# GAT's first edges by fp32 one-hots made from a broadcast of places, in blocks of 125 nodes and a written order

## The chip, the cores and the metric

The kernel runs on one core of one Trainium2 chip. The metric is the device time of one execution in microseconds (us), lower is better; where several runs are given, their median. The core has engines that run beside each other, each through its own queue in order: PE (matmuls, with its weight loads shown apart as PEld), DVE (elementwise and reductions), ACT (elementwise, with functions), POOL (here: indirect DMAs, that is gathers and scatters by a list of rows) and SP (here: only DMA issues). DMA queues of SP, ACT and POOL share 16 DMA engines. SBUF is the memory on the chip, PSUM the one that PE writes to.

## The reference

There are 3125 nodes with 64 features and 103125 edges (50000 random pairs in both directions and a loop for each node), sorted by destination. Two residual blocks follow one another, each on relu(layernorm(x)):

```python
def gin_layer(x, src, dst, ew, w1, b1, w2, b2):
    msg = x[src] * ew[:, None]
    agg = segment_sum(msg, dst)
    h = relu((agg + x) @ w1 + b1)
    return h @ w2 + b2            # three of these, relu between them

def gat(x, src, dst, W, a_src, a_dst, bias):
    xw = (x @ W).reshape(n, H, C)                 # H = 8 heads
    logits = leaky_relu(al_s[src] + al_d[dst], 0.2)   # al: xw times a_src or a_dst
    e = exp(logits - segment_max(logits, dst)[dst])
    alpha = e / segment_sum(e, dst)[dst]
    return segment_sum(alpha * xw[src], dst) + bias
```

In the second block x is embedded to 128 features (with a time embedding of node_vec), and three GAT layers follow (128 to 256, 256 to 256, 256 to 128), each with a dense residual, a batch norm over the nodes and a silu; a last matmul goes back to 64. Everything is fp32.

## The kernel before, in words

Nodes stand in NT = 25 blocks of P = 128 (3200 places for 3125 nodes). The program runs these stages one after another.

**search** and **slots** (L623, L749) sort the edges into slots: a row of slots for each destination. `weigh(t)` (L817) finds, for a block of destinations, which slots name the same source, adds up their weights and gives the first of them a cell in a dense adjacency of 3200 x 3200 fp32 in DRAM; `put(t)` (L836) has POOL scatter these values one column of 128 cells at a time (`scatter`, L941; 857 DMAs in the profile). Then, for each destination and each block of sources, the first edge is taken out (`tops`, L860 to L870) and its place within the block kept in `lane`; what is left of the edges goes into lists (`rank`, L711; the destinations in an order of falling list length, in `perm`, and the sources in `idx`). The lists' lengths per block are fixed: MORE = (44, 24, 22, 21, 20, 19, 18, 17, 17, 16, 16, 15, 15, 14, 14, 13, 13, 13, 12, 11, 11, 10, 10, 8, 7), 400 in all. A flag then selects `fast` (L1290).

**hots** (L923) makes the one-hots of the first edges: for each destination block t, DVE compares `lane` with a row of numbers (L929, bf16, 128 x 3200), PE transposes the 25 squares, ACT copies them from PSUM and SP writes 0.8 MB to `hot[t]` in DRAM. It stands before GIN in the text, but nothing keeps the scheduler from running it beside GIN.

**gin** (L954), three times: the adjacency (41 MB) is loaded in 75 pieces by SP (225 in all) and multiplied by the node features on PE (L977).

**gat** (L991), three times, with D = 256, 256 and 128. A preparation computes xw with the logits' source parts beside it (W = D + 8 columns), writes it to DRAM as `tab`, splits it into three bf16 terms that add up to the fp32 value (`split`: ACT one copy, DVE three operations per five blocks), and computes the dense residual into DRAM. `add_edges` (L1058) does the edges, in a loop over the destination blocks t:

- `gather(t, s0, n, rows)` (L1071): for each source block s, three bf16 matmuls with the one-hot as the stationary operand give in PSUM the row of xw that each destination's first edge names (L1078); ACT copies two of them at a time to SBUF (L1079). A 26th "source block" is an identity, for the node itself. The 26 are done as 12, 12 and 2, in three large tiles that rotate.
- `weigh(t)` (L1085) adds the logits, and `exps` (L1176) takes maximum, exponential (ACT, L1182) and sum. `add_part` (L1102) multiplies the rows by the exponentials (`times`, L1100), folds the 12 into 6 (L1105) and adds these up in PSUM with an identity matmul (L1107).
- `others(t)` (L1111) has POOL fetch the rows of the list, one indirect DMA of 128 rows for each list place (L950), into tiles of SG = 8 places, six of them in rotation. `add_others` (L1125) computes their logits (L1128), exponentials and products (L1100), sums all places in PSUM (L1139), and a scatter by POOL brings the sum to `more`, in the nodes' own order.

The lists are worked off in step with the blocks (`due`, a share of the list work by each t). The tile framework's scheduler decides the order on each engine. It places semaphores by the tiles' dependences, and a tile of a rotation can be written again when its last reader is done. `close_rows` (L1185) joins `res` and `more` by their maxima and sums, adds the dense part and applies batch norm and silu.

Of the kernel before, what the change touches and what calls it, by code (L numbers as in the profile page):

```python
# [22 lines left out]
NT = 25  # L23
NP = NT * P
# [573 lines left out]
class Fast(Base):  # L598
# [8 lines left out]
    def __init__(self, base, ctx):  # L607
        self.__dict__.update(base.__dict__)
        self.keep = ctx.enter_context(self.tc.tile_pool(name="keep", bufs=1))

        self.node = self.keep.tile([P, NT, 4], I32, name="node")
        self.place = self.keep.tile([P, NT], I32, name="place")
        self.flag = self.keep.tile([1, 1], I32, name="flag")

        self.bad = self.keep.tile([P, 8], F32, name="bad")
        self.edges = self.tc.dram_tile([P * J + P, 2], F32, name="edges")

        self.adj = self.tc.dram_tile([NP * NP + NC * P, 1], F32, name="adj")

        self.hot = self.tc.dram_tile([NT, P, NP], BF16, name="hot")  # L620
        self.adj_rows = self.adj[: NP * NP].rearrange("(s d) f -> s (d f)", d=NP)
# [89 lines left out]
    def rank(self, sp, ps, count, caps, bad):  # L711
# [12 lines left out]
        for c0 in range(0, BINS * NT, BLK):  # L724
            w = min(BLK, BINS * NT - c0)
            for lhs, o in ((self.after, ahead), (self.ones, tot)):
                pp = ps.tile([P, BLK], F32, name="pp", bufs=4)
# [21 lines left out]
    def slots(self):  # L749
# [11 lines left out]
        self.identb = keep.tile([P, P], BF16, name="identb")  # L761
        nc.vector.tensor_copy(self.identb, self.ident)
# [5 lines left out]
        with tc.tile_pool(name="slots", bufs=1) as sp, tc.tile_pool(name="slots_ps", bufs=1, space=PSUM) as ps:  # L768
# [35 lines left out]
            for t, c in enumerate(spans):  # L804
# [5 lines left out]
            earlier = sp.tile([P, CMAX, CMAX], F32, name="earlier")  # L810
            wide = [P, CMAX, CMAX]
            nc.vector.tensor_tensor(
                earlier, k[:, :, None].to_broadcast(wide), k[:, None, :].to_broadcast(wide), op=ALU.is_gt
            )
            celli, val = self.celli, self.val

            def weigh(t):  # L817
# [7 lines left out]
                    same, src[:, c, None].to_broadcast(wide), src[:, None, c].to_broadcast(wide), op=ALU.is_equal  # L825
                )
                nc.vector.tensor_tensor(part, same, earlier[:, :n, :n], op=ALU.mult)
                again = sp.tile([P, CMAX], F32, name="again", bufs=2)[:, :n]
                nc.vector.reduce_sum(again, part, axis=AX.X)
                nc.vector.scalar_tensor_tensor(again, again, 0.0, taken[:, c], op0=ALU.is_equal, op1=ALU.mult)  # L830
                nc.vector.tensor_tensor(again, again, cell[:, c], op=ALU.mult)
                nc.vector.tensor_tensor(celli[:, c], again, spare[:, c], op=ALU.add)
                nc.vector.tensor_tensor(same, same, wgt[:, None, c].to_broadcast(wide), op=ALU.mult)
# [16 lines left out]
            nc.gpsimd.iota(ends, pattern=[[P, NT]], base=P + 1, channel_multiplier=0, allow_small_or_imprecise_dtypes=True)  # L850
# [3 lines left out]
            nc.vector.tensor_mul(key, key, taken)  # L854
            NF = (NT + 7) // 8 * 8
# [6 lines left out]
            for t, c in enumerate(spans):  # L862
# [4 lines left out]
                    u, key[:, None, c].to_broadcast(wide), ends[:, :, None].to_broadcast(wide), op=ALU.is_lt  # L867
                )
                nc.vector.tensor_tensor(u, u, key[:, None, c].to_broadcast(wide), op=ALU.mult)
# [15 lines left out]
            pt = ps.tile([1, P], F32, name="pt1")  # L885
# [14 lines left out]
            lanes = sp.tile([P, NT, NF], F32, name="lanes")  # L900
            nc.sync.dma_start(lanes, tops_d.rearrange("(t p) f -> p t f", p=P))
# [4 lines left out]
            nc.gpsimd.iota(block, pattern=[[P, NT]], base=1, channel_multiplier=0, allow_small_or_imprecise_dtypes=True)  # L906
            nc.vector.tensor_copy(int_[:, :, :NT], lanes[:, :, :NT])
            nc.vector.tensor_scalar(int_[:, :, :NT], int_[:, :, :NT], SHIFT, None, op0=ALU.arith_shift_right)
            nc.vector.tensor_copy(self.lane, int_[:, :, :NT])
            nc.vector.tensor_sub(self.lane, self.lane, block[:, None, :].to_broadcast([P, NT, NT]))  # L910
            nc.vector.memset(self.void, 0.0)
            nc.vector.tensor_scalar(self.void[:, :, :NT], self.lane, 0.0, NEG, op0=ALU.is_lt, op1=ALU.mult)
# [7 lines left out]
            nc.vector.tensor_scalar(off, src, 0.0, float(NP + 1), op0=ALU.is_equal, op1=ALU.mult)  # L920
            nc.vector.scalar_tensor_tensor(self.idx, src, -1.0, off, op0=ALU.add, op1=ALU.add)

    def hots(self, pool, ps):  # L923

        nc = self.nc
        for t in range(NT):
            oh = pool.tile([P, NT, P], BF16, name="oh", bufs=2)
            wide = [P, NT, P]
            nc.vector.tensor_tensor(  # L929
                oh, self.lane[:, t, :, None].to_broadcast(wide), self.iota[:, None, :].to_broadcast(wide), op=ALU.is_equal  # L930
            )
            by_src = pool.tile([P, NP], BF16, name="by_src", bufs=2)
            for s0 in range(0, NT, 8):
                n = min(8, NT - s0)
                pt = ps.tile([P, 8, P], BF16, name="pt", tag="mm")
                for i in range(n):
                    nc.tensor.transpose(pt[:, i], oh[:, s0 + i], self.identb)
                nc.scalar.copy(by_src[:, s0 * P : (s0 + n) * P], pt[:, :n].rearrange("p s d -> p (s d)"))
            nc.sync.dma_start(self.hot[t], by_src)

    def scatter(self, table, rows, group="place"):  # L941
        for row, idx in rows:
# [3 lines left out]
            self.tc.declare_no_dep(st.ins, group=group, reason="each has a row of its own")  # L946
            self.tc.add_to_no_dep_group(group, st.ins)
# [43 lines left out]
    def gat(self, layer, K, D, xt, yt):  # L991
# [4 lines left out]
        tab = tc.dram_tile([NP + 1, W], F32, name=f"tab{layer}")  # L996
# [4 lines left out]
        with ExitStack() as ctx:  # L1001
            pool = ctx.enter_context(tc.tile_pool(name=f"gat{layer}", bufs=1))
            ps = ctx.enter_context(tc.tile_pool(name=f"gat_ps{layer}", bufs=2, space=PSUM))

            split = [pool.tile([P, NT, W], BF16, name=f"split{i}") for i in range(3)]
            ald = pool.tile([P, NT, H], F32, name="ald")
            stat = pool.tile([P, NT, 2 * H], F32, name="stat")
            back = pool.tile([P, NT, 2 * H], F32, name="back")
            gb, ab, bg, bb = (self.column(pool, name(n), KO) for n in ("gat_b", "adj_b", "bn_g", "bn_b"))
            bias = pool.tile([P, KO], F32, name="bias")  # L1010
            nc.scalar.dma_start(tab[NP:], self.none[:, 256 - D :])
            with tc.tile_pool(name=f"gat_a{layer}", bufs=2) as ap:
# [13 lines left out]
                for t0 in range(0, NT, S):  # L1026
                    row = ap.tile([P, S, W], F32, name="row")
                    for t in range(t0, t0 + S):
                        p = ps.tile([P, BLK], F32, name="pw", tag="mm")[:, : W + H]
                        for k in range(K):  # L1030
                            nc.tensor.matmul(p, xt[k][:, t * P : (t + 1) * P], gw[:, k], start=k == 0, stop=k == K - 1)
                        nc.scalar.copy(row[:, t - t0], p[:, :W])
                        nc.scalar.copy(split[0][:, t], p[:, :W])
                        nc.vector.tensor_copy(ald[:, t], p[:, W:])
                    nc.sync.dma_start(tab[t0 * P : (t0 + S) * P].rearrange("(t p) d -> p t d", p=P), row)
                    self.store_rows(ald_d, ald, t0, t0 + S)
                    left = ap.tile([P, S, W], F32, name="left", bufs=1)
                    part = [a[:, t0 : t0 + S] for a in split]
                    nc.vector.tensor_sub(left, row, part[0])
                    nc.vector.tensor_copy(part[1], left)  # L1040
                    nc.vector.tensor_sub(part[2], left, part[1])
# [11 lines left out]
            with tc.tile_pool(name=f"gat_sum{layer}", bufs=2) as io:  # L1053
                self.add_edges(io, ps, layer, D, xt, yt, split, ald, stat, tab, ald_d, res, more)
            with tc.tile_pool(name=f"gat_io{layer}", bufs=2) as io:
                self.close_rows(pool, io, ps, D, yt, stat, back, dense, res, more, bg, bb, xt[0])

    def add_edges(self, io, ps, layer, D, xt, yt, split, ald, stat, tab, ald_d, res, more):  # L1058
# [5 lines left out]
        two = xt[0].bitcast(BF16)  # L1064
        hot = [two[:, :NP], two[:, NP:], io.tile([P, NP], BF16, name="hot", bufs=1)]
        tiles = [a[:, : HALF * W].rearrange("p (s w) -> p s w", w=W) for a in (xt[1], yt[0], yt[1])]

        def load(t):
            nc.sync.dma_start(hot[t % 3], self.hot[t])

        def gather(t, s0, n, rows):  # L1071
            for i in range(0, n, 2):
                g = ps.tile([P, 2, BLK], F32, name="g", tag="g")
                for j in range(2):
                    s = s0 + i + j
                    one = hot[t % 3][:, s * P : (s + 1) * P] if s < NT else self.identb
                    for k, a in enumerate(split):
                        nc.tensor.matmul(g[:, j, :W], one, a[:, min(s, t) if s == NT else s], start=k == 0, stop=k == 2)  # L1078
                nc.scalar.copy(rows[:, i : i + 2], g[:, :, :W])  # L1079

        def parts(t):
            last = io.tile([P, 2, W], F32, name="last")
            return [(0, HALF, tiles[2 * t % 3]), (HALF, HALF, tiles[(2 * t + 1) % 3]), (2 * HALF, 2, last)]

        def weigh(t, now):  # L1085
            l = io.tile([P, NS, H], F32, name="l1")
            wide = [P, NS, H]
            nc.vector.tensor_tensor(
                l, self.void[:, t, :, None].to_broadcast(wide), ald[:, t, None, :].to_broadcast(wide), op=ALU.add
            )  # L1090
            for s0, n, rows in now:
                nc.vector.tensor_tensor(l[:, s0 : s0 + n], l[:, s0 : s0 + n], rows[:, :, D:], op=ALU.add)  # L1092
            self.lrelu(l, l)
# [260 lines left out]
```

## Time and profile before

| | us |
|---|---|
| median of 5 runs | 5112.81 (5109.6 to 5129.89) |
| the profiled execution, its own time | 5133.85 |
| its span in the profile | 5132.0 |
| POOL busy | 2686.1 (52%) |
| PE busy | 2240.1 (44%) |
| DVE busy | 2030.3 (40%) |
| ACT busy | 866.8 (17%) |
| moved by DMA | 465.63 MB, mean 91 GB/s |

The stages, from the start of the span: search and slots to about 894 (POOL's scatters go on to 1550), GIN from 1557 to 1979, GAT layers from about 2016 (edges 2064 to 3072, 3204 to 4200 and 4330 to 5075), the end at 5132.

How to read the profile: a row of groups gives line, engine, operation, output and inputs, their shapes and the count, then the busy time in us and the mean of one in ns, then the engine's idle time just before such operations and what ended most of it ("<-PE pa L1139": an operation of PE on tile `pa` at line 1139). A row of the stages gives the window, its length, and for each engine the busy time with the number of records, then the mean clock granted to PE as a share of the full one, the busy share of the DMA engines and the rate. A row of the timeline gives start, length, engine, line and operation, and in brackets the idle time before it. PE's records overlap each other, so that the mean duration of one is longer than the distance between two.

### The profile page before, as it was taken

What the parts mean: (1) busy time and instruction counts of PE and PEld (TensorE: products, weight loads), DVE (VectorE), ACT (ScalarE), POOL (GpSimd) and SP (SyncE); (2) the same over time, 40 slices, a digit from 0 to 9 for tenths busy, and PEclk for the clock granted to TensorE, in tenths of its full rate; (3) what the DMA queues carried; (4) which work ended last, traced back from release to release, by engine and by line L of the source; (5) the groups of instructions that cost most, each with busy time, mean ns of one, the idle gap of its engine ahead of it and who ended that gap; (6) DMA issues with size and microseconds to landing.
All of it is one profiled execution on the core that took longest, in us unless ns stands there. A gap on an engine that the chain in (4) does not pass through costs nothing. (4 is left out here: it accounts for less than half of the span.)

```text
span 5132.0 us, 36988 instructions
## 1 busy us (share of the span) xinstructions
PE 2240.1 (44%) x13235; PEld 1663.6 (32%) x13235; DVE 2030.3 (40%) x3336; ACT 866.8 (17%) x1812; POOL 2686.1 (52%) x2350
## 2 busy tenths in 40 slices
PE   0000000000007897466755566466665655364464
PEld 0000000000003433345544444345544544254454
DVE  3571930100005203345554445355554544243345
ACT  0000000000005302212212214122221214121122
POOL 2486687777770000565575440655565431666663
PEclk9555555555558997778877878778877877677787
DMA  9100000000007994432232223422322224322222
GB/s 382 51 1 7 1 0 14 2 1 1 1 0 264 363 377 160 113 86 86 84 94 77 74 62 128 100 81 85 89 86 83 64 73 127 52 76 70 69 75 70
DMA packets 235781, 465.63 MB, mean 91 GB/s; under 512 B 102719, under 2 KB 145858, under 8 KB 232386
## 3 DMA queue, kind: packets, MB, share of 16 engines
q1 hardware_dynamic: 113606, 252.99, 14.0%
q0 software_dynamic: 89424, 157.97, 12.5%
q10 hardware_dynamic: 32556, 52.20, 2.8%
q8 instruction: 106, 1.74, 0.1%
q14 instruction: 89, 0.73, 0.0%
HBM read 363.97 MB, written 99.01 MB: 90 GB/s over the span
## 5 line engine op out<-in xcount | busy, mean ns | idle before, releaser
L950 POOL DMA_INDIRECT rows<-tab,idx x1200 | 1467.4, 1223 | 867.0 <-PE pa L1139 510.4
L943 POOL DMA_INDIRECT adj<-val,celli x857 | 924.9, 1079 | 347.0 <-issue 259.9
L1078 PE MATMUL g<-split,xt 128*128 128x264 bf16 (+1 forms) x3825 | 506.8, 288 | 651.5 <-ACT xt L1079 399.3
L1078 PEld LDWEIGHTS <-xt 128*128 128x128 bf16 x3825 | 380.9, 109 | 769.3 <-issue 689.2
L1079 ACT COPY xt<-g 128x528 f32<-128x528 f32 (+1 forms) x900 | 465.4, 527 | 734.1 <-PE g L1078 288.6
L977 PE MATMUL pa<-adj_t,h 128*64 128x512 f32 (+1 forms) x1050 | 274.6, 560 | 667.0 <-DMA adj_t<-adj 666.6
L950 POOL DMA_INDIRECT at<-ald,perm x75 | 73.8, 984 | 924.7 <-DVE l L1092 532.5
L1139 PE MATMUL pa<-rows,ident 128*128 128x256 f32 (+1 forms) x2400 | 503.3, 365 | 42.3 <-ACT o L1140 25.1
L1128 DVE TENSOR_TENSOR l<-rows,at 128x64 f32<-128x64 f32 (+4 forms) x180 | 38.8, 216 | 1065.0 <-DMA rows<-tab,idx 1019.6
L1139 PEld LDWEIGHTS pa<-rows,ident 128*128 128x128 f32 x2400 | 428.0, 206 | 91.8 <-ACT o L1140 32.9
L1107 PE MATMUL pa<-xt,ident 128*128 128x256 f32 (+1 forms) x1800 | 409.4, 380 | 61.1 <-DVE xt L1105 50.6
L1100 DVE TENSOR_TENSOR xt<-xt,e 128x3072 f32<-128x3072 f32 (+1 forms) x150 | 416.4, 2817 | 0.0
L1078 PE MATMUL g<-split,hot 128*128 128x264 bf16 (+1 forms) x1800 | 245.5, 293 | 378.4 <-ACT xt L1079 199.1
L1107 PEld LDWEIGHTS pa<-xt,ident 128*128 128x128 f32 x1800 | 330.8, 213 | 112.3 <-DVE xt L1105 63.5
L977 PEld LDWEIGHTS pa<-adj_t,h 128*64 128x64 f32 x1050 | 82.8, 136 | 807.7 <-issue 743.1
L1078 PEld LDWEIGHTS <-hot 128*128 128x128 bf16 x1800 | 181.9, 111 | 435.8 <-issue 395.2
L1100 DVE TENSOR_TENSOR rows<-rows,e 128x2048 f32<-128x2048 f32 (+8 forms) x180 | 289.3, 1632 | 0.0
L175 DVE TENSOR_SCALAR em_t<-em_t,wave 128x512 f32<-128x512 f32 (+1 forms) x7 | 3.8, 545 | 659.0 <-DMA em_t<-in_node_vec 658.9
L1105 DVE TENSOR_TENSOR xt<-xt 128x1536 f32<-128x1536 f32 (+1 forms) x150 | 216.6, 1486 | 0.0
L1182 ACT ACTIVATE e<-l 128x208 f32<-128x208 f32 (+17 forms) x150 | 51.5, 344 | 972.8 <-DVE l L1181 923.1
L728 PE MATMUL pp<-oh,after 128*128 128x512 f32 (+1 forms) x16 | 9.6, 687 | 419.4 <-DVE row L880 416.7
L182 PE MATMUL p<-em_k,L_gnn_te_w 128*128 128x512 f32 (+1 forms) x14 | 8.6, 704 | 348.6 <-ACT em_k L180 348.6
(255 smaller groups left out, 2526.5 us busy)
## 6 DMA issues: line engine op xcount, KB each, us to landing
adj_t<-adj SPq DMA_DIRECT2D x150, 512.0 KB
adj_t<-adj SPq DMA_DIRECT2D x75, 576.0 KB
xt<-hot SPq DMA_DIRECT2D x51, 800.0 KB
adj<-zero ACTq DMA_DIRECT2D x25, 1600.0 KB
hot<-by_src SPq DMA_DIRECT2D x25, 800.0 KB
hot<-hot SPq DMA_DIRECT2D x24, 800.0 KB
rows<-tab,idx POOLq DMA_INDIRECT x1200
adj<-val,celli POOLq DMA_INDIRECT x857
```

What stands on the lines that cost most here:

```text
L728: nc.tensor.matmul(pp[:, :w], lhs, flat[:, c0 : c0 + w], start=True, stop=True)
L943: st = self.nc.gpsimd.indirect_dma_start(out=table, out_offset=bass.IndirectOffsetOnAxis(ap=idx, axis=0), in_=row, in_offset=None)
L950: self.nc.gpsimd.indirect_dma_start(out=out, out_offset=None, in_=table, in_offset=bass.IndirectOffsetOnAxis(ap=idx, axis=0))
L977: nc.tensor.matmul(pa[i * D0 : (i + 1) * D0, c : c + w], h[:, s], tiles[i][:, c : c + w], start=s0 == 0, stop=s0 + i >= NT - 2 and i == 1,)
L1078: nc.tensor.matmul(g[:, j, :W], one, a[:, min(s, t) if s == NT else s], start=k == 0, stop=k == 2)
L1079: nc.scalar.copy(rows[:, i : i + 2], g[:, :, :W])
L1100: nc.vector.tensor_tensor(r, r, e[:, s0 : s0 + n, :, None].to_broadcast([P, n, H, C]), op=ALU.mult)
L1105: nc.vector.tensor_add(rows[:, :m, :D], rows[:, :m, :D], rows[:, m:n, :D])
L1107: nc.tensor.matmul(pa, self.ident, rows[:, j, :D], start=s0 + j == 0, stop=s0 + n == NS and j == m - 1)
L1128: nc.vector.tensor_tensor(l[:, k0 : k0 + n], rows[:, :n, D:], at[:, None, :].to_broadcast([P, n, H]), op=ALU.add)
L1139: nc.tensor.matmul(pa, self.ident, rows[:, k, :D], start=k0 + k == 0, stop=k0 + k == MORE[t] - 1)
L1182: nc.scalar.activation(e, l, AF.Exp)
```

## The change

**Slots.** The tiles that are compared or multiplied over (source ids, weights, keys, the order of slots) are copied to PSUM by ACT, and the DVE operations of `weigh` and `tops` take one input from there. The first slot among equals is found by a maximum over the order, not by a table of earlier slots. `rank`'s PSUM tiles are two in place of four.

**One-hots.** Blocks of nodes become Q = 125 (25 x 125 = 3125). PE transposes `lane` once, it goes to DRAM as bf16, and for each t SP loads one row of 3200 places, broadcast to 125 partitions; DVE compares it with the partition's own number, and ACT's queue stores the fp32 result, 1.6 MB for each t. `tc.no_sync_barrier()` between this and GIN keeps each engine's instructions of the two apart, in each engine's own order.

**GAT.** xw stays in SBUF as fp32 (`xw`), the three bf16 terms go, and a gathered pair is one fp32 matmul. Logits and exponentials live in PSUM. Leaky relu is two operations (`bend`) in place of one. `tc.manual_schedule()` makes the order of each engine that of the text in `add_edges`: a list is fetched and its logits weighed ahead of the last, small part of block t, its products and sums come after that block's result is copied out, and its own copy out after the next block's logits. The last part is no longer folded. Scatters to `more` no longer declare themselves independent. Each stage has PSUM pools of its own; the zero rows behind the table's end are written by ACT's queue.

```diff
+            src_p = ps.tile([P, NC], F32, name="src_p")
+            nc.scalar.copy(src_p, src)
+            wgt_p = ps.tile([P, NC + CMAX], F32, name="wgt_p")
+            nc.scalar.copy(wgt_p[:, :NC], wgt)
...
                 nc.vector.tensor_tensor(
-                    same, src[:, c, None].to_broadcast(wide), src[:, None, c].to_broadcast(wide), op=ALU.is_equal
-                )
-                nc.vector.tensor_tensor(part, same, earlier[:, :n, :n], op=ALU.mult)
+                    same, src[:, c, None].to_broadcast(wide), src_p[:, None, c].to_broadcast(wide), op=ALU.is_equal
+                )
+                nc.vector.tensor_tensor(part, same, order_p[:, None, :n].to_broadcast(wide), op=ALU.mult)
...
     def hots(self, pool, ps):
...
+            for i in range(n):
+                nc.tensor.transpose(pt[:, i, :Q], self.lane[:Q, t0 + i], self.ident[:Q, :Q])
+            nc.scalar.copy(lanes[:, t0 : t0 + n, :Q], pt[:, :n, :Q])
+        nc.sync.dma_start(lane_d.rearrange("t s d -> s t d"), lanes)
...
         for t in range(NT):
-            oh = pool.tile([P, NT, P], BF16, name="oh", bufs=2)
...
+            row = pool.tile([P, NP], BF16, name="row", bufs=2)[:Q]
+            nc.sync.dma_start(row, flat[t].partition_broadcast(Q))
+            one = pool.tile([P, NP], F32, name="one", bufs=2)[:Q]
+            nc.vector.tensor_scalar(one, row, own[:Q], None, op0=ALU.is_equal)
+            nc.scalar.dma_start(self.hot[t], one)
...
             with tc.tile_pool(name="hots", bufs=1) as hp:
                 k.hots(hp, k.ps)
+
+        tc.no_sync_barrier()
+        with tc.tile_pool(name="fgin_ps", bufs=2, space=PSUM) as k.ps:
...
-                        nc.scalar.copy(row[:, t - t0], p[:, :W])
-                        nc.scalar.copy(split[0][:, t], p[:, :W])
+                        nc.scalar.copy(xw[:, t], p[:, :W])
...
-                    nc.vector.tensor_sub(left, row, part[0])
-                    nc.vector.tensor_copy(part[1], left)
-                    nc.vector.tensor_sub(part[2], left, part[1])
...
+                name=f"gat_ps_sum{layer}", bufs=1, space=PSUM
+            ) as ps, tc.manual_schedule():
...
-        two = xt[0].bitcast(BF16)
-        hot = [two[:, :NP], two[:, NP:], io.tile([P, NP], BF16, name="hot", bufs=1)]
+        hot = [xt[0]] + [io.tile([P, NP], F32, name=f"hot{i}", bufs=1) for i in range(2)]
...
-                    one = hot[t % 3][:, s * P : (s + 1) * P] if s < NT else self.identb
-                    for k, a in enumerate(split):
-                        nc.tensor.matmul(g[:, j, :W], one, a[:, min(s, t) if s == NT else s], start=k == 0, stop=k == 2)
+                    one = hot[t % 3][:Q, s * P : s * P + Q] if s < NT else self.ident[:Q, :Q]
+                    nc.tensor.matmul(g[:Q, j, :W], one, xw[:, t if s == NT else s], start=True, stop=True)
...
+        def bend(l, n):
+            z = io.tile([P, RMAX, H], F32, name="z")[: l.shape[0], :n]
+            nc.vector.tensor_scalar(z, l, SLOPE, None, op0=ALU.mult)
+            nc.vector.tensor_tensor(l, l, z, op=ALU.max)
...
+                if i == 2:
+                    weighed = None
+                    while done < NT and due[done] <= t * due[-1] / NT:
+                        if weighed:
+                            end_others(*add_others(*weighed))
+                        weighed = weigh_others(done, *others(done))
+                        done += 1
                 add_part(pa, e, *now[i])
...
-            while done < NT and due[done] <= (t + 1) * due[-1] / NT:
-                add_others(done, *others(done))
-                done += 1
-            if more_:
-                now, e = nxt, weigh(t + 1, nxt)
+            added = weighed and add_others(*weighed)
+            if ahead:
+                now, e = nxt, weigh(t + 1, nxt)
+            if added:
+                end_others(*added)
```

`logits` places `l` and `e` of a block or a list in one PSUM bank; `weigh_others` is the first half of the old `add_others` (logits and exponentials), `add_others` the second (products and sums), `end_others` its last two lines.

## The prediction

> **What bounds the kernel now.** I read the busy shares first, then the span cut into stages, then the groups by idle time, then the timeline of one GAT iteration. No engine is busy more than 52% of the span (POOL), so the bound changes from stage to stage. The stages (columns: PE, PE weight loads, DVE, ACT, POOL busy with counts, granted clock, DMA share, GB/s):
>
> ```profile
> 548.00:1550.00 1002.00, 3.68 (x9) 1.21 (x8) 168.96 (x215) 8.75 (x12) 778.76 (x732) 0.50 0.03 3
> 1557.00:1720.00 163.00, 134.79 (x916) 62.99 (x916) 97.45 (x59) 99.52 (x130) 0.00 (x0) 0.95 0.90 314
> 1720.00:1960.00 240.00, 224.93 (x1049) 91.46 (x1048) 11.43 (x32) 16.38 (x29) 0.00 (x0) 1.00 0.99 383
> 2064.00:3072.00 1008.00, 618.23 (x3408) 493.18 (x3408) 490.75 (x572) 224.78 (x432) 572.64 (x450) 0.80 0.30 82
> 3204.00:4200.00 996.00, 612.76 (x3374) 486.92 (x3372) 490.63 (x573) 223.28 (x427) 561.44 (x448) 0.80 0.30 82
> 4330.00:5075.00 745.00, 379.82 (x3325) 353.49 (x3322) 305.29 (x576) 142.83 (x417) 490.40 (x450) 0.73 0.27 69
> ```
>
> Row one is POOL scattering adjacency cells alone: 732 DMAs in 1002 us. Rows two and three are GIN, on the DMA engines (share 0.90 to 0.99), with the one-hots in row two. The last three are the edge stages of the GAT layers, 2749 us together, in which PE, DVE and POOL are each 41 to 66% busy: they wait for one another. The groups say for what:
>
> ```profile
> L950 POOL DMA_INDIRECT rows<-tab,idx x1200 | 1467.4, 1223 | 867.0 <-PE pa L1139 510.4
> ...
> L1139 PE MATMUL pa<-rows,ident 128*128 128x256 f32 (+1 forms) x2400 | 503.3, 365 | 42.3 <-ACT o L1140 25.1
> L1128 DVE TENSOR_TENSOR l<-rows,at 128x64 f32<-128x64 f32 (+4 forms) x180 | 38.8, 216 | 1065.0 <-DMA rows<-tab,idx 1019.6
> ```
>
> DVE stands 1020 us at L1128, waiting for rows that POOL has not fetched; POOL stands 510 us until PE has summed (L1139) and so freed a buffer. One turn of this:
>
> ```profile
> 2409.07 2.75 PE L1107 MATMUL pa<-xt,ident 128*128 128x256 f32 x12
> ...
> 2412.77 8.80 PE L1139 MATMUL pa<-rows,ident 128*128 128x256 f32 x40
> ...
> 2416.66 3.12 POOL L950 DMA_INDIRECT rows<-tab,idx  x1 [13.35 <-PE pa L1139]
> ...
> 2433.20 0.23 DVE L1128 TENSOR_TENSOR l<-rows,at 128x64 f32<-128x64 f32 x1 [6.41 <-DMA rows<-tab,idx]
> ```
>
> It takes about 44 us (2402 to 2446). DVE has L1128 of the next list queued ahead of the next block's work, so the block waits too.
>
> One trap: **an fp32 matmul is two records.** L1139 has 2400 records for 3 x 400 fetched rows. So 40 records in 8.8 us are 20 matmuls at 0.44 us, and the 12 of L1107 run from 2409.07 to the next group at 2411.66, 0.43 us each. A bf16 matmul of 264 columns is one record: 30 in 3.88 us, 0.129 each.
>
> **The change, part by part.**
>
> *Slots.* POOL waits 51 us for DVE (L832) and starts its last 732 scatters at 548. Each should take 1.274 us (0.97 and 0.30 of issue), 933 in all; 69 more are lengthening by DVE:
>
> ```profile
> 890.10 0.78 DVE L916 TENSOR_SCALAR int<-int 128x1200 int32<-128x1200 int32 x1
> 890.57 1.24 POOL L943 DMA_INDIRECT adj<-val,celli  x1 [0.31 <-issue]
> ...
> 895.78 3.48 DVE L929 TENSOR_TENSOR oh<-lane,iota 128x3200 bf16<-128x3200 f32 x1
> 896.38 3.73 POOL L943 DMA_INDIRECT adj<-val,celli  x1 [0.30 <-issue]
> ```
>
> Beside an operation that reads two SBUF tiles a scatter lasts as long as that operation; beside the reduction at 894.04 (one SBUF input) the next took 0.97. The change gives those operations one PSUM input. No row shows that case beside POOL; ends: 0 and all 69 come off. I take all, as for the reduction, and 28 for the earlier start, since the first 175 scatters (199 us busy, 1.14 each) shorten to 0.97 (ends 0 and 51). Together -97.
>
> *One-hots, moved.* They ran inside GIN (L929 onward, on PE, ACT and SP) and now run from about 800, on all engines ahead of the new barrier, beside the scatters. They move 25 x 0.8 MB in and 25 x 1.6 MB out, 60 MB; at 383 to 423 GB/s (GIN's row; the zeroing at 45 to 90 us) about 150 us. PE, ACT, DVE and SP stood still there until about 1557, so for them it is hidden. POOL is not: its packets share the DMA engines. The nearest row is the zeroing, 1.6 MB writes beside POOL's row gathers: 1150 and 1152 packets, alternating, one POOL DMA every 3.2 us. Ends: nothing lost, or 3.2 us instead of 1.27 for 150 us, which is 47 scatters instead of 118, 71 x 1.27 = 90. I take 90. What lies queued behind the barrier is GIN, which needs the scatters anyway. GIN's start: -97 + 90 = **-7**.
>
> [...]
>
> *GIN* now loads the adjacency alone: 3 x 41.5 MB at the 383 GB/s of row three is 325 us, with a head of 5 and a tail of 20 as now 350, against 422 (1557 to 1979): **-72** (ends -45, -90).
>
> *Preparation and closing*: DVE's splits (1.5 + 0.85 + 1.5 us per 5 blocks) and ACT's second copy (0.38 per block) go, but lie mostly beside PE and stores, and the first hot load doubles to 1.6 MB. **-5** over the layers (ends -30, +15).
>
> *Edge stages, D = 256.* A gathered (t, s) pair costs one fp32 matmul, 0.44 us, for three bf16, 0.387: PE gets slower here. Per iteration 26 gathers, 14 part sums and about 16 list sums: 56 x 0.435 = 24.4 us of PE. DVE has 3.3 + 1.7 + 3.3 + 1.7 (parts), 0.7 (last), 4.6 (two groups of eight rows at 2.28), 1.8 and 3.1 (logits), 0.9 (sums of exponentials), 21 us. POOL: 18 x 1.27 = 23. All three are near equal, so the written order decides. POOL now runs a list ahead and DVE meets the list in mid-iteration, so I expect the row waits to go; what is late next is the exponential of the list's logits, which in ACT's order stands behind the last gather copy. From the end of the first part's add: PE does 6 part sums, 12 gathers, 6 part sums, 2 gathers (26 x 0.435 = 11.3), ACT a copy 0.6 and the exponential 0.35, handovers 0.6: 12.9 us, of which DVE works only 6.8. Then DVE alone: 0.4, 0.7, 4.6, next logits 3.1 with a wait of 0.44 and a sum of 0.53, next first part 5.0: 14.8. Cycle 27.7 us. Twenty iterations with a list 554, five without (40 matmuls and the logits, 21) 105, two second lists 16, the long first two lists (44 and 24 rows) 16, first gather and logits 18, last lists 17, hot load 5: 731, say 735. Ends: 690 (matmul at 0.40, the fastest weight loads of 0.186 twice) and 830 (0.50). Against 1008 and 996: **-273 and -261**.
>
> [...] The trace has the fp32 price already: weight loads of 0.192 to 0.214 us against 0.106 to 0.109 for bf16, so a record every 0.22. [...]
>
> *D = 128*: DVE's part halves and PE is the bound: 25 x 24.4 = 609, waits for the logits 1.7 x 25 = 43, ends 33: 685 (625 to 740), against 745: **-60**.
>
> **Sum.** 5133.85 (the profiled execution; span 5132.0) -7 -72 -5 -273 -261 -60 = 4456. The median of the runs, 5112.81, is 21 lower, so **4440** as a median.
>
> **Rivals.**
> 1. *The engines overlap fully* (chance 0.13): each layer takes its busiest engine, 610 to 620. For it: each has its own queue and POOL six buffers. Against: the exponential's place in ACT's order. 5133.85 - 84 - 388 - 376 - 130 = 4156.
> 2. *The row waits stay in part* (0.14): L1128 cost 392 us in layer 0; if a third remains, since DVE's written order still stops there with the block's work behind it, D = 256 takes 850 and layer 2 730: 4730.
> 3. *PSUM inputs do not free POOL* (0.12): the change does not do what it says. The 69 stay, and POOL keeps its 1.30 per fetch (450 x 1.30 = 585, near PE's 608), some 10 more a layer: 4456 + 99 = 4555.
> 4. *Slower* (0.04): PE at the low clock. The slowest weight load in the trace is 0.338; two records make 0.72 us, 56 x 0.72 = 40 an iteration, about 1130, 1130 and 1070: 5630. It decides from 0.6 us a matmul on, where the three layers are back at about 2830. Against: clock 1.00 in row three with PE 94% busy.
>
> **The numbers.** The forecast has 0.55, and 0.02 is for what I do not see. The range 4240 to 4740 takes in the bounds of the terms (matmul, scatters, GIN) and rivals 2 and 3; it leaves out 1, 4 and the rest, 0.19. A measurement here tells about 0.3% from no change: faster 0.94, same 0.01, slower 0.05 (rival 4 and a hundredth of the rest).
>
> **What would show it.** Right: scatters ending near 1545 and at 0.97 except while one-hots are written; GIN near 350; edge stages of 735, 735, 685 with PE 80% busy and ACT's exponential waited for by DVE once per iteration; L1128's successor with almost no wait for rows. Wrong: gather matmuls far from 0.44, PE's clock under 0.8, or DVE waiting for row DMAs.

## The result, and the profile after

| | before | after |
|---|---|---|
| median on the first chip | 5109.55 us (45 runs) | 5159.72 us (24 runs) |
| span of the profiled execution | 5132.0 | 5166.6 |

The ratio is **1.0096 [1.0082, 1.0111]**: one per cent slower, where 4440 us was forecast. How large the change's effect is depends on the chip: on another chip the same two kernels took 4591.5 and 4993.8 us, a ratio of **0.9199 [0.9169, 0.9229]** (run e9_after). So two questions stand: what the forecast lacked on every chip, and what the first chip adds.

The stages of the kernel after, first chip (columns as in the prediction's first fence). The six rows are the stores of one-hots beside the scatters, GIN, the edges of the first layer, the stretch between the edges of two layers, and the edges of the other two:

```profile
977.00:1449.00 472.00, 0.00 (x0) 0.00 (x0) 45.24 (x24) 0.00 (x0) 326.64 (x306) 0.50 0.33 119
1577.00:1905.00 328.00, 307.66 (x1349) 118.99 (x1350) 12.86 (x36) 20.57 (x36) 0.00 (x0) 0.99 0.97 374
2028.00:2910.00 882.00, 699.42 (x2800) 548.11 (x2800) 497.46 (x597) 225.98 (x427) 470.91 (x449) 0.88 0.38 113
2910.00:3117.00 207.00, 87.85 (x359) 67.81 (x360) 52.64 (x107) 44.79 (x92) 0.97 (x1) 0.69 0.30 92
3117.00:4003.00 886.00, 698.74 (x2785) 547.06 (x2783) 495.62 (x596) 224.94 (x424) 465.36 (x448) 0.88 0.39 112
4180.00:5066.00 886.00, 469.05 (x2771) 424.80 (x2771) 315.88 (x589) 149.43 (x423) 432.33 (x448) 0.70 0.30 80
```

The windows of the edges lie up to 9 us off the first gather and the last sum, which bound these stages below. GIN is as forecast (328 us for 350). The first row is not: the one-hots take 472 us at 119 GB/s. The fourth row took 134 us before. And the third layer, with half the columns, takes as long as the first two. The groups:

```profile
L964 POOL DMA_INDIRECT rows<-tab,idx x1200 | 1211.7, 1010 | 876.6 <-PE pa L1173 418.6
...
L1093 PE MATMUL g<-xw,hot 125*125 125x264 f32 (+1 forms) x2400 | 561.8, 385 | 272.4 <-issue 200.6
L1173 PE MATMUL pa<-rows,ident 128*128 128x256 f32 (+1 forms) x2400 | 565.3, 406 | 95.0 <-DVE rows L1128 50.2
...
L1228 DVE TENSOR_REDUCE o<-le 128x8 f32<-128x104 f32 (+16 forms) x75 | 21.9, 292 | 913.2 <-ACT le L1227 717.8
```

A fetch takes 1.010 us where it took 1.223, so POOL is freed as forecast. The 1020 us that DVE stood for rows are 42 here (L1160, L1128's successor), and 225 in e9_after (point 5 of the account below). In their place DVE stands 718 us for ACT's exponential of the list, L1227: the wait that the prediction named as next, but far more of it.

In the profiled executions the stages add up. GIN starts 15 us later (1577 for 1562) and takes 79 less; the four stretches ahead of, between and behind the edges take 123, 206, 177 and 93 us for 95, 134, 114 and 66, 190 more; the edge stages take 882, 895 and 886 for 1005, 1006 and 743, 91 less. 15 - 79 + 190 - 91 = +35, and the spans differ by 34.6.

### The profile page after: what moved, and what is told of

The parts are those of the page before. It is cut to its first block, busy times and chain, and to the rows that moved or that the text cites. A ratio compares the mean times of both kernels' runs of the same rounds, so it can differ in the third digit from the quotient of the medians.

```text
span 5166.6 us, 32313 instructions
## 1 busy us (share of the span) xinstructions
PE 2475.2 (48%) x10835; PEld 1846.5 (36%) x10835; DVE 1979.5 (38%) x3392; ACT 793.9 (15%) x1652; POOL 2378.3 (46%) x2350
## 5 line engine op out<-in xcount | busy, mean ns | idle before, releaser
L964 POOL DMA_INDIRECT rows<-tab,idx x1200 | 1211.7, 1010 | 876.6 <-PE pa L1173 418.6
L1093 PE MATMUL g<-xw,hot 125*125 125x264 f32 (+1 forms) x2400 | 561.8, 385 | 272.4 <-issue 200.6
L1094 ACT COPY xt<-g 125x528 f32<-125x528 f32 (+1 forms) x900 | 472.2, 529 | 863.0 <-PE g L1093 462.3
L1093 PEld LDWEIGHTS g<-xw,hot 125*125 125x125 f32 x2400 | 420.5, 206 | 391.7 <-issue 228.1
L1128 DVE TENSOR_TENSOR xt<-xt,le 125x3072 f32<-125x3072 f32 (+1 forms) x150 | 421.7, 2812 | 0.0
L1093 PE MATMUL g<-xw,xt 125*125 125x264 f32 (+1 forms) x1350 | 317.7, 386 | 164.5 <-issue 79.3
L1137 PE MATMUL pa<-xt,ident 125*125 125x256 f32 (+1 forms) x1800 | 374.6, 362 | 16.9 <-DVE xt L1135 15.8
L1137 PEld LDWEIGHTS pa<-xt,ident 125*125 125x125 f32 x1800 | 318.3, 205 | 57.1 <-issue 11.2
L1093 PEld LDWEIGHTS g<-xw,xt 125*125 125x125 f32 x1350 | 237.0, 207 | 233.2 <-issue 124.6
L1128 DVE TENSOR_TENSOR rows<-rows,le 128x2048 f32<-128x2048 f32 (+8 forms) x180 | 284.5, 1629 | 0.0
L1135 DVE TENSOR_TENSOR xt<-xt 125x1536 f32<-125x1536 f32 (+1 forms) x150 | 224.0, 1493 | 5.1
```

The lines of the kernel that those rows point to most:

```text
L964: self.nc.gpsimd.indirect_dma_start(out=out, out_offset=None, in_=table, in_offset=bass.IndirectOffsetOnAxis(ap=idx, axis=0))
L1093: nc.tensor.matmul(g[:Q, j, :W], one, xw[:, t if s == NT else s], start=True, stop=True)
L1094: nc.scalar.copy(rows[:, i : i + 2], g[:Q, :, :W])
L1128: nc.vector.tensor_tensor(r, r, e[:, s0 : s0 + n, :, None].to_broadcast([*r.shape[:3], C]), op=ALU.mult)
L1135: nc.vector.tensor_add(rows[:, :m, :D], rows[:, :m, :D], rows[:, m:n, :D])
L1137: nc.tensor.matmul(pa, self.ident[:Q, :Q], rows[:, j, :D], start=s0 + j == 0, stop=s0 + n == NS and j == m - 1)
```

## The experiments

Each ratio is to the kernel before, run on the same chip. The runs fell on six chips. On that of e5 to e8 the kernel before takes 5114 us, near the 5110 of the first result (it may be the same chip), on the five others 4994 to 5000.

**The DMAs of 125 partitions.** In row one the DMA engines carry only the one-hots and POOL's scatters, and no other engine has much to do, and yet their share is 0.33. e1_split makes each DMA of 125 partitions two:

```diff
+    def halves(self, engine, out, in_):
+        for a, b in ((0, 112), (112, Q)):
+            engine.dma_start(out[a:b], in_[a:b])
...
-            nc.scalar.dma_start(self.hot[t], one)
+            self.halves(nc.scalar, self.hot[t], one)
...
-            nc.sync.dma_start(hot[t % 3][:Q], self.hot[t])
+            self.halves(nc.sync, hot[t % 3][:Q], self.hot[t])
```

and likewise for the row, `tab`, `res`, `back` and the loads of the closing.

> The changed kernel with every DMA over 125 partitions issued as two, over 112 (7 x 16) and over 13; same bytes, same results. Theory A (a transfer over 125 partitions keeps only about 5 of the 16 DMA engines busy: share 0.33 and 130 GB/s while the one-hots are written, 0.36 and 113 GB/s in the first closing, against 0.9 and 350 GB/s in the closing of before): the one-hots' stage falls from 472 us to about 170; closing plus preparation from 206, 176 and 88 us to about 135, 125 and 57; the edge stages stay near 882, 896 and 890 but for earlier hot loads. Total 5160 -> about 4990. Rival (the slow closings come from their PSUM pool and the written order, not from the transfers): one-hots faster at most, total within 20 us of 5160.

4387.8 us, ratio 0.8778 [0.876, 0.8795]; a second time, on another chip (e11_split), 4393.8, 0.8799 [0.8765, 0.8833]. The stages of one-hots, whole DMAs in e9_after and split ones in e1_split:

```profile
842.00:1308.00 466.00, 0.00 (x0) 0.00 (x0) 45.31 (x24) 0.00 (x0) 327.66 (x307) 0.50 0.33 121
```
```profile
841.00:1032.00 191.00, 0.00 (x0) 0.00 (x0) 45.75 (x24) 0.00 (x0) 142.70 (x117) 0.50 0.93 297
2660.00:2806.00 146.00, 77.51 (x356) 58.69 (x356) 52.10 (x107) 44.71 (x91) 0.97 (x1) 0.79 0.50 130
```

466 us at a share of 0.33 become 191 at 0.93, with the same bytes. That two DMAs run side by side can't be the reason, since the one of 112 carries nine tenths of the bytes. The last row is the stretch between layers, without its last 2 us: 205 us in e9_after (206 in after), 148 here. On e5's chip the split was made in parts: one-hots' rows and stores alone (e6), the loads of one-hots in the edges alone (e7), all the others alone (e8).

> The changed kernel itself again, beside the kernel before on the same chip, as the base for the three runs with it. In the first four runs the kernel before took 5000 us, not 5110, its twin with the slots edit showed only 2 PE signals over 2 us late (148 in the first profile of before, 166 in the first profile of the change), and the run with pauses took 0.937 of before. Theory C (late PE signals come with the chip, not with the change, and struck the change's written order harder): where before takes about 5000 the change takes about 4650, ratio 0.92 to 0.94. Rival (the pauses removed them, so theory B): ratio near 1.01, late signals again in long POOL runs.

> Of the 112 + 13 split only the one-hots' stage: the 25 broadcast loads and the 25 stores of 1.6 MB. Theory A, by the profiles of the full split and of the pause run: the stage 466 -> about 190 us, last scatter about 33 us earlier (1495 -> 1462), total 33 less than the change. If instead the denser one-hots cost POOL its 90 us of my forecast, the last scatter comes no earlier and the total is the change's.

> Of the split only the 75 loads of one-hots in the GAT layers (1.6 MB each, about 12.5 us on a third of the engines). Theory A with these loads off the path (an iteration takes 28 us, a load is issued one ahead): edge stages within 10 us of the change's, total within 25. Rival (the long packets stand ahead of POOL's row fetches on the few engines they use, so fetches land late): 20 to 50 us less per layer.

> Of the split only the row transfers around the edge stages: stores of xw, of the logits' parts and of the sums, and the loads of closing. Theory A: the stretches before the layers and the tail from 122, 205, 180, 93 us to about 102, 148, 128, 71, total 150 less than the change. Rival: nothing.

Unsplit (e5) 1.0107 [1.0063, 1.0152]; e6 1.0024 [0.9996, 1.0051], e7 1.0122 [1.0083, 1.0162], e8 0.9827 [0.9777, 0.9877]. In e6 the last store is issued at 1177 instead of 1450 and the scatters 34 us earlier (1533 for 1567). In e8 the four stretches take 100, 152, 131 and 70 us, 148 less than the 601 of e5. The loads inside the edges are hidden by other work: no gain.

**Long runs of POOL.** On the first chip the edge stages stand still in places. From the timeline of after:

```profile
2532.11 0.61 PE L1093 MATMUL g<-xw,xt 125*125 125x264 f32 x2
2532.33 0.41 PEld L1093 LDWEIGHTS g<-xw,ident 125*125 125x125 f32 x2
2532.55 0.61 PE L1093 MATMUL g<-xw,ident 125*125 125x264 f32 x2
2533.14 0.95 POOL L964 DMA_INDIRECT rows<-tab,idx  x1 [0.30 <-issue]
...
2549.75 0.60 ACT L1094 COPY last<-g 125x528 f32<-125x528 f32 x1 [17.70 <-remote]
2550.25 0.27 ACT L1227 ACTIVATE le<-le 128x128 f32<-128x128 f32 x1
2550.55 0.29 DVE L1228 TENSOR_REDUCE o<-le 128x8 f32<-128x128 f32 x1 [31.88 <-ACT le L1227]
```

By the profile, in which the ends of matmuls are modelled, PE has the last gather done at 2533.2, but ACT's copy of it starts at 2549.75: PE's semaphore events arrive at 2542.7, 2546.9 and 2549.7. The profile calls such a wait "remote". Behind it stands the exponential, and behind that DVE. In the GAT of this profile 166 events of PE come over 2 us after PE's last finished instruction, up to 51 us; in the turn shown POOL is issuing fetch after fetch meanwhile. The waits of the kernel before (first fence) and of after (second), first chip, total us, times, longest:

```profile
ACT xt L1079 <- remote: 179.4, 30, 18.4
DVE row L880 <- remote: 38.8, 14, 5.3
ACT last L1079 <- remote: 33.9, 6, 13.0
```
```profile
ACT xt L1094 <- remote: 275.1, 52, 15.6
ACT last L1094 <- remote: 212.4, 25, 29.5
ACT o L1177 <- remote: 78.8, 5, 49.5
...
DVE row L886 <- remote: 43.3, 17, 3.3
DVE key L880 <- remote: 25.5, 9, 5.2
```

The late events are not PE's alone. The DVE rows of both fences are in the slots stage, and the events that end these waits are DVE's own: in after DVE stands 135 us there for its own earlier operations (eight such groups, of which two are shown). In e9_after none of these waits appears.

The theory was that an unbroken run of POOL's DMAs causes them. e2_pause puts other work between POOL's fetches, after each group of at most eight (`rest` is a tile of 128 x 2048 in fp32):

```diff
+                nc.gpsimd.memset(rest, 0.0)
```

> The changed kernel with one POOL memset of 128 x 2048 (about 1.8 us by the 2.76 us of the 128 x 3200 one) after each group of up to eight row fetches; 60 a layer, about 110 us of POOL time more per layer. Theory B (in the edge stages PE's semaphore updates come late, by up to 50 us, once POOL has issued some 20 indirect DMAs in one unbroken run; ACT and DVE then stand still): the late updates go, edge stages from 882, 896, 890 to about 800, 810, 740, total about 4860 to 4950. Rival (the late updates are PE's own, from its clock or from fp32 matmuls, or POOL is the bound): nothing gained, POOL's extra 110 us per layer show, total 5160 to 5400.

> The change as it is, base of this group. The two groups so far ran on two chips: before 5000 us on one, 5114 on the other, where the change took 5156 and 162 PE signals came over 2 us late. If before takes about 5110 here: the change 5150 and about 160 late signals. If before takes about 5000: theory C says 4650 and next to none late; its rival says 5050 (ratio 1.01 everywhere).

e2_pause took 4678.0, 0.9365 [0.934, 0.939], on e1's chip, with edges of 771, 768 and 697 us. But e9_after, the change itself on a third chip, has 768, 779 and 613 and **no remote wait at all**, with two events of PE over 2 us late instead of 166, though in the GAT POOL's DMAs follow each other without a pause of 0.6 us for up to 402 at a time, against 49 at most in after. So long runs are not enough to make events late; what decides came with the chip, or with the time at which it was used, and e2_pause tells nothing of a cure. The pause was run again, to meet a chip with late events (e10 0.9393 [0.9361, 0.9425], e13 0.9383 [0.9362, 0.9405], e16 0.9369 [0.9342, 0.9396], e17 0.9381 [0.9341, 0.9421], on three more chips), and with the split (e3 0.8975 [0.8948, 0.9003], e12 0.8986 [0.8956, 0.9016]).

> Both edits of the two runs above together. Theories A and B both right and independent: about 5160 - 170 - 250 = 4740. Only A: about 4990. Only B: about 4900. If slow hot loads are what makes POOL's runs hurt (their packets ahead of the fetches'), less than the sum: the pause adds nothing to the split.

> The pauses once more, for a chip with late events (there before takes about 5110 and the change 1.01 of it). Theory B (they need an unbroken POOL run of some 20 indirect DMAs): late PE events fall from about 160 to under 40, edge stages to 780, 780, 710, total 0.94 to 0.96 of before. Rival (any POOL DMAs beside PE make them, broken or not): they stay over 100, total 1.0 to 1.05. On a chip without them: 0.94 of before, as twice before, and nothing is told.

None met one. Where events are in time the pause only costs: 0.90 for 0.88 with the split, all of it on POOL's own time (third layer 697 to 699 for 614).

**Slots alone.** e4_slots is the kernel before with the part "Slots" of the change and nothing else (the fence of the diff on slots).

> The kernel before with the slots part of the change alone (PSUM inputs for the comparisons, first slot by a maximum); one-hots, GIN and GAT as before. My step said 97 us off the end of the scatters (28 from an earlier start, 69 from scatters no longer lengthened): total 5110 -> about 5015, scatters at 0.97 us throughout, last at about 1452 instead of 1549. Rival (PSUM inputs do not free POOL): scatters still 1.06 us in the mean, total within 30 us of 5110.

4949.7, 0.9895 [0.9876, 0.9914]: 51 us, not 97. A scatter takes 0.995 us on average (1.079 in the first profile of before), so the PSUM inputs do free POOL. This run is also the only trace of the old GAT on a chip without late events: edges 1001, 1004 and 685 us.

**Parts of the edge step.** Both on top of the split: e14 takes `tc.manual_schedule()` away, so that the scheduler orders the engines; e15 puts the logits and exponentials into SBUF.

```diff
-            ) as ps, tc.manual_schedule():
+            ) as ps:
```
```diff
-            a = ps.tile([P, BLK], F32, name=name, tag=name)[:rows]
...
+            l, e = (io.tile([P, n * H], F32, name=f"{x}{name}", bufs=2)[:rows] for x in "le")
```

> The split kernel without the written order in the edge stages: the scheduler orders them, as in before (DVE takes the next list's logits ahead of the next block's work again). If the written order is what removed the row waits: edge stages of D = 256 back from 765 to 900 to 1000, total (chip without late events) from 4390 to about 4800. Rival (fp32 one-hots, PSUM logits and free POOL did it): within 50 us of 4390.

> The split kernel with logits and exponentials of the edge stages in SBUF again. My forecast: with two SBUF inputs the products lengthen POOL's fetches, 1.02 -> about 1.25 to 1.30 us in the mean, but POOL (450 x 1.6 = 700 at the worst) stays under the DVE and PE chain of 28 us an iteration for D = 256: 10 to 40 us a layer more there, 50 to 90 in layer 2, total 4390 -> 4470 to 4550. Rival (PSUM inputs free nothing): fetches and total unchanged. Other rival (it was the core of the gain): D = 256 layers back over 900.

e14: 4483.5, 0.898 [0.896, 0.8999], edges 796, 799 and 652. The written order is worth 2 per cent, some 95 us; most of the gain is not the order's. e15: 4521.2, 0.9041 [0.9018, 0.9063], edges 802, 800 and 677. Its fetches, beside those of e1_split (second fence):

```profile
L970 POOL DMA_INDIRECT rows<-tab,idx x1200 | 1549.8, 1292 | 453.6 <-issue 313.1
```
```profile
L970 POOL DMA_INDIRECT rows<-tab,idx x1200 | 1227.6, 1023 | 578.2 <-issue 308.2
```

1.292 us against 1.023: this is rival 3's mechanism, reversed. The edit costs some 130 us; it also changes what DVE and ACT read and write, so how much of that is POOL's own isn't shown.

**The wait that is next.** The prediction's chain of an iteration has ACT's exponential of the list behind the last gather's copy. e18 keeps the split and issues the list's logits ahead of that gather:

```diff
-                if ahead:
-                    gather(t + 1, *nxt[i])
                 if i == 2:
                     weighed = None
...
+                if ahead:
+                    gather(t + 1, *nxt[i])
```

> The split kernel with one step of the written order moved: the list's logits and exponential are issued ahead of the last gather's copy instead of behind it. Theory (the forecast's chain step: the list's exponential on ScalarE, queued behind the copy of the last gather, is what is late next): VectorE's waits for ScalarE's exponential in the first layer (166 us in 25 waits in the split kernel) fall under 60 us, an iteration goes from 28 us to 24 to 25, the two layers of 256 columns from 760 to 770 each to some 690, and the total to some 4230, 0.84 to 0.855 of the kernel before. Rival (TensorE's own chain, its matmuls at the clock of 0.5 after each pause, is as long): the wait moves to TensorE, the layers stay within 15 us of 760 to 770 and the total within 30 us of 4390, 0.87 to 0.885.

**4209.7 us, 0.8429 [0.8414, 0.8444]**, the fastest version; the edges take 680, 680 and 611 us, for 769, 763 and 614 in e1_split. One turn, first of e11_split and then of e18:

```profile
2126.59 0.60 ACT L1100 COPY last<-g 125x528 f32<-125x528 f32 x1 [2.88 <-PE g L1099]
2127.09 0.31 ACT L1233 ACTIVATE le<-le 128x168 f32<-128x168 f32 x1
2127.42 0.33 DVE L1234 TENSOR_REDUCE o<-le 128x8 f32<-128x168 f32 x1 [9.58 <-ACT le L1233]
...
2158.53 0.32 DVE L1234 TENSOR_REDUCE o<-le 128x8 f32<-128x160 f32 x1 [8.65 <-ACT le L1233]
```
```profile
2135.14 0.30 ACT L1233 ACTIVATE le<-le 128x160 f32<-128x160 f32 x1
2135.47 0.32 DVE L1234 TENSOR_REDUCE o<-le 128x8 f32<-128x160 f32 x1 [4.41 <-ACT le L1233]
...
2138.12 0.60 ACT L1100 COPY last<-g 125x528 f32<-125x528 f32 x1 [2.69 <-PE g L1099]
...
2161.97 0.32 DVE L1234 TENSOR_REDUCE o<-le 128x8 f32<-128x152 f32 x1 [4.29 <-ACT le L1233]
```

The exponential now comes ahead of the copy, DVE's wait halves (166.0 us in 25 waits of the first layer become 80.9, not under 60) and the turns shown take 26.5 us for 31.1 (their lists begin with 20 rows and 21; with the same lists as in the turn of e11_split e18 takes 26.9). The rival, that PE takes the wait over, falls: no cause of PE's waits in that layer sums to more than 10.3 us, and its clock is 0.98 for 0.95. Half of DVE's wait is left: the exponential still stands behind the copies of the gather ahead of it, the last of which ends at 2135.24 where the logits were done at 2131.06.

## Why the prediction was wrong

The terms of the sum, beside what the profiles give. Without late events the only old edges are those of e4_slots, so the right-hand columns are differences to it (its kernel before took 5000.3 us, that of e9_after 4993.8).

| step | forecast | e9_after | e1_split | e18 |
|---|---|---|---|---|
| slots (e4 to before) | -97 | -51 | -51 | -51 |
| one-hots beside scatters | +90 | +69 | +38 | +36 |
| GIN | -72 | -83 | -83 | -83 |
| preparation and closing | -5 | +184 | +28 | +26 |
| edges | -594 | -530 | -543 | -718 |

The last four of e9_after sum to -360; the spans differ by 361.

1. **"60 MB; at 383 to 423 GB/s ... about 150 us" failed.** It was 472 us at 119 GB/s (466 at 121 in e9_after). The rate came from rows with 128 partitions, where the DMA engines have a share of 0.99 (row three of the prediction's stages); in the stage of 125 it is 0.33, and 0.93 with the same bytes as 112 and 13 (e1_split). The forecast had no row with 125 partitions. 0.33 x 16 is 5.3, and the about 5 engines of e1_split's theory A are no more than that: which engines are busy, and why, no run here shows. The +90 was near in size (+69), but only a part of it for its reason (point 3).
2. **"Preparation and closing ... -5 (ends -30, +15)" failed by 190 us**, the largest miss that every chip shows. Of its DMAs only the first load of one-hots was costed, though the partitions of the others go from 128 to 125. The split gives 156 of it back; the +28 that are left were not traced further.
3. **"71 x 1.27 = 90. I take 90" has POOL's queue alone and nothing for DVE's comparisons.** While one-hots are made, the trace of after has

```profile
1237.01 2.22 POOL L956 DMA_INDIRECT adj<-val,celli  x1 [0.51 <-issue]
1237.22 1.89 DVE L950 TENSOR_SCALAR one<-row,own 125x3200 f32<-125x3200 bf16 x1 [16.38 <-issue]
```

   a scatter of 2.22 us beside the comparison of 1.89, for 0.97: 25 x 1.25 = 31 us. The prediction's fence on slots has a pair like it, a scatter of 1.24 beside the TENSOR_SCALAR of 0.78 at 890.10. The queue's cost comes beside this. In the stage of one-hots of e9_after POOL waits for its own earlier scatters,

```profile
POOL adj L956 <- DMA adj<-val,celli: 68.6, 82, 5.5
```

   which is 44 us more than the usual 0.30 apiece (43 in after). With split DMAs these waits are 16.8 us in 17, and the lengthening by comparisons stays at 30. The 3.2 us per POOL DMA beside the zeroing, from which the 90 came, were no price of a shared queue: POOL waits for DVE between any two of them there (2.41 us before the one at 45.29), and DVE for the rows.
4. **Slots: "I take all" was mis-sized**: 51 of 97. That scatters fall to the 0.97 of undisturbed ones came true nearly (0.995). Both its parts, the earlier start and the lengthening, were read from a profile with late events; which of them fell short isn't known, since there is no profile of the kernel before without late events.
5. **The edge stages of 256 columns were right in mechanism and, without late events, near in size**: 768 and 779 for 735 and 735. An fp32 gather matmul is two records (3900 of L1093 in after for 3 x 25 x 26), PE is busy for 671 of 767 us, the row waits went (10.6 and 24.9 us in e9_after), and the exponential was next: DVE waits for it 163.5 us in 25 waits in either layer, and e18 shows it by taking half of that away. With e18's order the two come to 680 and 680, 60 to 70 above rival 1.

   **The third layer, "PE is the bound: 25 x 24.4 = 609", is near in size (613 for 685) by luck.** Its row in e9_after, and the longest of DVE's waits there:

```profile
3879.00:4491.00 612.00, 409.24 (x2798) 378.79 (x2799) 318.16 (x595) 152.63 (x425) 435.24 (x449) 0.81 0.45 115
DVE le L1160 <- DMA rows<-tab,idx: 190.1, 35, 12.3
```

   PE is busy for 409 us: the 24.4 are those of 256 columns. POOL is the bound. Its 449 DMAs take 435 us, and with 0.30 of issue between two of them some 570, as the prediction's own 23 us of POOL an iteration make 575; DVE waits for rows, which the prediction gave as a sign of being wrong. The pauses agree: they cost time in this layer and not in the others.
6. **On the first chip the edge step failed**: 882, 895 and 886. Neither the forecast nor a rival had semaphore events that come late. The old edges on that chip lost nothing by them in the first two layers (1005 and 1006 for 1001 and 1004) and 58 us in the third; the new ones lose 503 together. From e9_after to after on the first chip the spans differ by 581: 72 in slots (where DVE stands for late events of its own: it is busy 124 us from 300 to 552 for 193, and the scatters end at 1565 for 1493), 4 in GIN, 503 in edges, 3 elsewhere. That the new order suffers more since a wait in it reaches DVE through ACT's queue within the same turn is argued from the timeline, not shown.

**Open:** what makes the events late on some chips, and whether shorter runs of POOL would cure it. Of the 166 in after 81 fall into runs of at least eight POOL DMAs without a pause of 0.6 us, and these runs fill 1668 us, about half of the GAT's time: no sign that the two go together. The late profiles also lack events. That of after has 3306 for the 3667 instructions of PE that send one, 2559 for DVE's 3035 and 1244 for ACT's 1590, that of e9_after as many as there should be, within 5; whether they were joined with later ones or lost to the profile isn't told. Neither the pause nor the full split nor e18 ran on such a chip, so what they are worth there wasn't tried.

The forecast was 0.868 of the median it started from. Without late events the change gives 0.92 (one chip), with its DMAs split 0.88 (two chips), and with one statement moved besides 0.843 (one chip).

## What to carry to other kernels

Before a tile's partitions are changed, look at every DMA that carries it: 125 rows in place of 128 cost some 200 us here (e9_after to e11_split, one chip), and two DMAs of 112 and 13 gave them back. When a forecast names the wait that will be next, look whether the change can be written so that it is not: moving one statement was worth 4 per cent, more than the whole written order. A result of one chip should be taken on a second one before it is explained: the same change gave 1.01 on the first chip and 0.92 in e9_after.

## What the runs showed of the hardware

- DMAs of 125 partitions moved 121 GB/s at a share of 0.33 (stage of one-hots, e9_after), the same bytes as 112 and 13 partitions 297 GB/s at 0.93 (e1_split).
- In the first result and on one of the six later chips semaphore events of PE come up to 51 us after the work that sends them (146 to 167 of them over 2 us late in the GAT of a run, 2 on the five other chips); in slots DVE waits for its own, up to 5.2 us at a time in after. The kernel before takes some 5110 us there and 4994 to 5000 elsewhere; the change's ratio is 1.01 there and 0.92 on the one other chip where it ran.
- With the exponentials in PSUM a fetch by POOL takes 1.023 us, with them in SBUF 1.292 (e1_split and e15).
